# Hawk and RWKV layer on one core: normalized x of six sequences turned in squares of 32 on VectorE and spread by transfers inside SBUF

## The chip, the cores and the metric

The kernel runs on one core of a Trainium2 chip. The metric is the device time of one execution in microseconds (us). Three runs of the kernel before took 638.42, 637.23 and 638.24 us; their median is 638.24.

## The reference, cut to what matters

Everything is float32. The input x has 8 sequences of 1024 tokens with 256 features. It is normalized over the features, and two branches that both start from the normalized xn are added to x:

```python
xn = _layernorm(x, axis=-1)
x = x + hawk(xn, ...) + rwkv(xn, ...)

# hawk: 256 -> 384 features, and back
gate = xn @ Wg.T ;  u = xn @ Wi.T
y = causal_conv(u, 4 taps) + conv_b
ig = sigmoid(y @ lru_Wi.T + bi) ;  rg = sigmoid(y @ lru_Wg.T + bg)
alpha = exp(-8 * softplus(lam) * rg)
h[t] = alpha[t] * h[t-1] + sqrt(1 - alpha**2 + 1e-6) * ig * y      # along the tokens
hawk = (gelu(gate) * h) @ Wo.T

# rwkv: tokens mixed with the token before
xr = mu_r * xn + (1 - mu_r) * xn_prev ;  xk = mu_k * xn + (1 - mu_k) * xn_prev
rwkv = sigmoid(xr @ W_r.T) * (relu(xk @ W_k.T)**2 @ W_v.T)
```

## The kernel before

**Layout.** x arrives with tokens on the 128 partitions (`xt`, eight tiles of 128 tokens with 256 features). Statistics and normalization work on that layout, one token a partition. The products need the features on the partitions: `xnT` holds xn turned over, two chunks of 128 features with 1024 tokens each, behind one column of zeros, so that a view one column to the left is the token before. `mix_before` (ScalarE) and `mix` (VectorE) make the mixed inputs `xk` and `xr` from the two views.

**How xn is turned.** `transposes` (L681) lets TensorE turn four 128x128 blocks into one PSUM bank, and `put_transposed` copies the bank into `xnT` (ScalarE, L700; for one half of the first sequence's blocks VectorE). A sequence takes four banks, so 16 transposes and four copies. `tp` puts the four pairs into the order of the work.

**The products.** Each large product is done in 2x2 blocks with seven products in place of eight. For this GpSimd makes sums of token halves (`token_sum`, L712) and of weights, and five steps of a `Group` let TensorE, ScalarE (`seed`, `five`, evictions) and VectorE (`fork_c`, `fork_d`) take turns on the PSUM banks. Groups are u (gates and u, three of them), k, r, v (the rwkv branch), l (the gates of the recurrence, three) and o (the hawk output).

**The order.** There is one loop over the sequences, s = 0 to 7. A turn of the loop makes u, k, r, v and l of sequence s, finishes the recurrence and o of sequence s - 1, and prepares sequence s + 1. The order is written out by hand and by a planner: `pe(f, ...)` gives TensorE its next place on a counter (one place is the time of one float32 product with 512 columns, two matmul records in the trace), and `at(t, f, ...)` puts a step of another engine at a time in the same unit. Where the table `PLACES` has a name, its number replaces t. Its four parts are "first" (s = 0), "second" (s = 1), "middle" (s = 2 to 6) and "last" (s = 7). In the end all steps are sorted by that number and issued. The numbers are thus not times on the chip: they fix the order on each engine's queue, transfers included, and the hardware waits for data where a step comes early.

```python
def pe(f, *args, length=1):
    steps.append((clock[0], len(steps), f, args, ""))
    clock[0] += length
```

**Transfers.** SP issues the loads of x (`load`, L647), the early weights and the stores of the result (L638, L778). GpSimd issues `add_x` (L766), which adds x from HBM into the buffer `sides`. In a middle turn the kernel before has the load of sequence s + 2 directly behind the transposes of s + 1 (L681), since both use `xt`. The convolution steps on VectorE are L795, the forks L474 and L482, the normalization on ScalarE L676, `mix_before` L723 and `mix` L729.

Of the kernel before, what the change touches and what calls it, by code (L numbers as in the profile page):

```python
# [10 lines left out]
ALU = mybir.AluOpType  # L11

P = 128
NT = 512
K = 4
# [21 lines left out]
        "early mix_before k 0": 4.0, "early token_sum x 0": 4.88, "early token_sum x 2": 5.16,  # L37
        "early mix_before k 1": 5.2, "early mix k 0": 6.32, "u0_0 evict 0 1": 6.43,
        "early mix_before r 0": 7.11, "early token_sum x 1": 7.82, "u0_0 evict 1 1": 8.36,
        "early mix k 1": 8.98, "u1 seed": 9.36, "conv_first 1": 10.05, "early token_sum k 0": 10.48,  # L40
        "second stats 0 1": 10.52, "u2 seed": 11.39, "second stats 1 1": 11.39,
        "early token_sum x 3": 11.65, "u1 five": 12.07, "second stats 2 1": 12.26, "u2 five": 12.75,
        "early token_sum k 1": 12.81, "second stats 3 1": 13.13, "u1 evict A 0 0": 13.44,
        "early token_sum k 2": 13.97, "early mix_before r 1": 14.12, "u1 fork_c": 14.36,
        "early token_sum k 3": 15.13, "second stats 4 1": 15.17, "conv_first 0": 15.35,
        "early halve v": 16.29, "u2 fork_c": 16.36, "k seed": 17.36, "early mix r 0": 18.02,
        "u1 fork_d": 19.52, "u2 evict A 0 0": 19.54, "early token_sum r 0": 19.68,
        "second stats 5 1": 20.32, "u1 evict C 0 1": 20.36, "early weight_sums l": 20.85,
        "k five": 21.05, "u2 fork_d": 21.36, "conv_first 2": 21.73, "second stats 6 1": 22.17,
        "u2 evict C 0 1": 23.07, "k evict A 0 0": 23.75, "early constant 0": 24.44,  # L50
        "early mix r 1": 24.45, "u1 late": 24.7, "r seed": 25.37, "k fork_c": 25.93,
        "early constant 1": 26.05, "early token_sum r 1": 26.09, "r five": 26.36,
# [5 lines left out]
        "r fork_d": 34.36, "k evict C 0 1": 34.78, "conv_rest 0 2": 34.93, "normalize 0 1": 36.27,  # L58
        "conv_rest 1 1": 36.33, "conv_rest 0 3": 37.82, "r evict C 0 1": 38.46, "r evict A 0 0": 39.15,
        "conv_rest 2 1": 39.31, "r evict B 1 0": 39.82, "r late": 40.5, "token_sum y 0": 40.8,  # L60
# [3 lines left out]
        "normalize 7 1": 46.3, "value 0": 46.89, "token_sum y 1": 46.89, "value 4": 47.56,  # L64
        "token_sum y 2": 47.88, "l0 evict A 0 0": 48.22, "value 2": 48.3, "token_sum y 3": 49.02,
        "l0 fork_c": 49.36, "value 6": 50.17, "early constant 4": 50.97, "add_x": 51.13,
# [6 lines left out]
        "early constant 18": 55.58, "put_transposed 0 1": 56.15, "put_transposed 1 1": 56.83,  # L73
        "token_sum x 0": 57.0, "mix_before k 0": 57.52, "token_sum x 2": 58.16, "l0 evict B 1 0": 58.74,
        "mix k 0": 59.32, "mix_before k 1": 59.54, "l1 evict A 0 0": 60.77, "token_sum x 1": 60.82,
        "l1 fork_c": 61.36, "mix_before r 0": 61.57, "token_sum k 0": 61.98, "mix k 1": 63.14,
        "l2 seed": 63.36, "l2 five": 64.36, "token_sum x 3": 64.64, "l0 evict D 1 1": 65.05,
        "l1 fork_d": 65.36, "token_sum k 1": 65.81, "mix_before r 1": 65.84, "mix r 0": 66.97,
        "decay 0": 67.07, "l1 evict C 0 1": 68.41, "token_sum k 2": 68.47, "decay_square 0": 69.21,
        "token_sum k 3": 69.63, "l2 evict A 0 0": 70.32, "l2 fork_c": 70.36, "decay 1": 71.12,  # L80
        "mix r 1": 71.17, "l1 evict B 1 0": 72.47, "decay_rest 0": 72.66, "decay 2": 73.27,
        "stats 0 1": 73.47, "l2 fork_d": 74.36, "l1 evict D 1 1": 74.61, "stats 1 1": 75.17,
        "decay_square 1": 75.41, "l2 evict C 0 1": 76.52, "decay_square 2": 77.32, "stats 2 1": 77.42,
        "stats 3 1": 78.29, "stats 4 1": 79.16, "stats 5 1": 80.03, "decay_rest 1": 80.91,
        "decay_rest 2": 85.37, "stats 6 1": 97.23, "stats 7 1": 108.37
    },
    "second": {
        "token_sum r 0": -1.17, "gated_input 0": -0.0, "token_sum r 1": 1.42, "u0 seed": 2.43,
        "token_sum r 2": 2.58, "u0 five": 3.11, "token_sum r 3": 3.75, "beta 0": 5.29,
        "gated_input 1": 5.71, "u0 evict A 0 0": 6.52, "u0 fork_c": 7.14, "beta 1": 7.2,  # L90
        "scaled_input 0": 7.94, "l2 evict B 1 0": 9.93, "recur 0 L": 10.18, "l2 evict D 1 1": 10.73,
        "u1 seed": 11.53, "scaled_input 1": 11.63, "k seed": 12.21, "u1 five": 12.89,
        "u0 fork_d": 13.06, "u0 evict C 0 1": 13.58, "recur 0 R": 13.86, "k five": 14.26,
        "u1 evict A 0 0": 14.94, "gated_input 2": 15.32, "conv_first 0": 15.63, "u1 fork_c": 16.74,
        "k evict A 0 0": 16.97, "k fork_c": 17.55, "gated_state 0": 18.35, "beta 2": 19.15,
        "recur 1 L": 19.77, "u2 seed": 20.38, "u0 evict B 1 0": 21.06, "token_sum o 0": 21.23,
        "u2 five": 21.74, "u1 fork_d": 21.96, "u1 evict C 0 1": 22.43, "scaled_input 2": 22.76,
        "conv_first 1": 23.11, "k fork_d": 24.19, "conv_first 2": 24.45, "recur 2 L": 24.99,
        "k late": 25.8, "u2 fork_c": 26.45, "recur 1 R": 27.25, "u2 evict A 0 0": 27.98,
        "k evict C 0 1": 28.66, "recur 2 R": 28.71, "gated_state 1": 30.14, "r seed": 30.58,  # L100
        "r five": 31.26, "u2 fork_d": 31.57, "token_sum v 2": 31.57, "k evict B 1 0": 31.94,
        "token_sum o 1": 32.73, "u1 evict B 1 0": 33.73, "token_sum v 0": 33.89, "r fork_c": 34.27,
        "u2 evict C 0 1": 34.3, "token_sum o 2": 34.79, "r evict A 0 0": 34.82, "u2 evict B 1 0": 35.44,
        "gated_state 2": 35.88, "u1 late": 36.12, "u2 late": 36.8, "r fork_d": 37.29,
        "token_sum v 1": 37.29, "r evict C 0 1": 37.48, "v seed": 38.36, "conv_rest 0 1": 38.44,
        "r late": 39.04, "v five": 39.72, "token_sum v 3": 39.93, "r evict B 1 0": 40.4,
        "conv_rest 0 2": 41.08, "deviation": 42.56, "v fork_c": 42.57, "token_sum o 3": 42.57,
        "v evict A 0 0": 43.36, "o seed": 43.36, "conv_rest 0 3": 44.16, "o five": 44.36,
        "v fork_d": 45.65, "token_sum y 0": 45.81, "v evict C 0 1": 46.45, "conv_rest 1 1": 47.24,
        "inverse 0 8": 48.73, "normalize 0 1": 49.26, "o fork_c": 49.36, "normalize 1 1": 49.84,  # L110
        "conv_rest 2 1": 49.93, "normalize 2 1": 50.34, "normalize 3 1": 51.03, "conv_rest 1 2": 51.33,
        "normalize 4 1": 51.73, "normalize 5 1": 52.43, "o fork_d": 52.81, "normalize 6 1": 53.12,
        "conv_rest 2 2": 53.61, "normalize 7 1": 53.83, "l0 seed": 54.53, "conv_rest 1 3": 55.11,
        "l0 five": 55.36, "conv_rest 2 3": 56.6, "token_sum y 1": 57.87, "o evict B 1 0": 57.87,
        "token_sum y 2": 58.88, "o evict C 0 1": 59.3, "token_sum y 3": 60.02, "v evict B 1 0": 60.11,
        "l0 evict A 0 0": 60.72, "l0 fork_c": 60.91, "l1 seed": 62.36, "v late": 62.51, "add_x": 63.47,
        "put_transposed 0 0": 63.86, "put_transposed 1 0": 64.44, "l1 five": 65.01,
        "put_transposed 0 1": 65.69, "l0 fork_d": 66.36, "put_transposed 1 1": 66.38,
        "token_sum x 0": 66.54, "mix_before k 0": 67.06, "token_sum x 2": 67.7, "mix_before k 1": 68.29,
        "mix k 0": 68.87, "l0 evict C 0 1": 69.51, "mix_before r 0": 70.31, "token_sum x 1": 70.36,  # L120
        "mix k 1": 71.53, "l0 evict B 1 0": 71.54, "l1 evict A 0 0": 72.36, "token_sum k 0": 73.02,
        "mix_before r 1": 73.16, "l1 fork_c": 73.36, "mix r 0": 74.19, "l0 evict D 1 1": 74.39,
        "l2 seed": 75.36, "token_sum k 1": 75.68, "decay 0": 76.05, "mix r 1": 76.85, "l2 five": 77.39,
        "decay_square 0": 78.07, "token_sum x 3": 78.35, "l1 fork_d": 78.35, "decay 1": 79.18,
        "stats 0 1": 79.43, "token_sum k 2": 79.51, "stats 1 1": 80.3, "l1 evict C 0 1": 80.52,
        "token_sum k 3": 80.67, "stats 2 1": 81.17, "decay_square 1": 81.32, "l2 fork_c": 82.36,
# [1073 lines left out]
```

## Time and profile before

| | |
|---|---|
| median of 3 runs | 638.24 us |
| profiled execution | 638.32 us |
| its span, first to last instruction | 636.6 us |
| granted TensorE clock, mean | 0.999 |
| one turn of the loop (transposes at 137.05, 214.08, 291.11) | 77.03 us |
| HBM read, written | 19.94 MB, 8.39 MB |
| mean DMA rate over the span | 45 GB/s |

The profile shows one execution. Its times count from the first instruction. A group of instructions has the line, the engine, the operation, "out<-in", the count, busy time, the mean of one, and the idle time of the engine just before them with what ended it. In a timeline, "[1.13 <-PE bank L395]" means that the engine sat idle for 1.13 us until TensorE had written that bank. A "q" behind an engine's name is its queue of DMA issues. The chain follows the work that ended last back from the end, step by step, to what released it.

### The profile page before, as it was taken

The numbers are of one execution on the slowest core, as the hardware profiler recorded it, in microseconds if no ns is written. First come the engines' busy times: TensorE is split into PE (matmuls) and PEld (weight loads), VectorE is DVE, ScalarE is ACT, GpSimd is POOL, SyncE is SP. The second block draws the span as 40 slices with busy tenths as digits, with TensorE's granted clock in tenths as the row PEclk, the third lists the DMA queues.
The fourth block names the chain that finished last, engine by engine and source line by source line (L and its number), as shares of the span: only waits on it lengthen the run. The fifth ranks groups of instructions, "written<-read, shape, count | busy, mean of one in ns | idle before, by whom it ended". The sixth has DMA issues, their size and how long they took to land.

```text
span 636.6 us, 7412 instructions
## 1 busy us (share of the span) xinstructions
PE 628.3 (99%) x2632; PEld 379.3 (60%) x2632; DVE 510.1 (80%) x644; ACT 484.4 (76%) x693; POOL 328.0 (52%) x227
## 2 busy tenths in 40 slices
PE   9999999999999999999999999999999999999997
PEld 4466445964469544795447854487445974457466
DVE  4768697978889688886798867978789877689695
ACT  3995999669994699937999289981999739994870
POOL 5984833669044780547606475083831749617000
PEclk9999999999999999999999999999999999999999
DMA  7200500043000710008000070001700023000403
GB/s 265 67 1 9 124 0 1 1 103 97 0 1 1 154 45 2 0 1 199 0 1 2 30 169 0 0 2 42 158 0 1 1 75 58 0 2 1 66 28 106
DMA packets 27366, 28.80 MB, mean 45 GB/s; under 512 B 961, under 2 KB 26817, under 8 KB 27329
## 3 DMA queue, kind: packets, MB, share of 16 engines
q1 hardware_dynamic: 18592, 19.53, 9.6%
q0 software_dynamic: 8320, 8.39, 8.5%
q8 instruction: 21, 0.34, 0.2%
q10 hardware_dynamic: 416, 0.41, 0.2%
q14 instruction: 17, 0.13, 0.1%
HBM read 19.94 MB, written 8.39 MB: 44 GB/s over the span
## 4 chain that ended last, share of the span: by engine, by line
PE 95%; ACT 1%; DVE 0%; issue 0%; DVEq 0%; ACTq 0%
PE bank L389 65%; PE bank L395 24%; PE bank L739 4%; PE bank L681 2%; ACT g L555 0%; ACT L659 0%; ACT L555 0%; ACT L344 0%; DVE bank L474 0%; ACT bank L466 0%; ACT five L471 0%; DVE side L776 0%; DVEq L1195 0%; ACT std L659 0%; DVE std L666 0%
## 5 line engine op out<-in xcount | busy, mean ns | idle before, releaser
L389 PE MATMUL bank<-y,w_l 128*128 128x512 f32 x288 | 137.9, 593 | 0.0
L795 DVE SCALAR_TENSOR_TENSOR y<-u,par,y 128x1024 f32<-128x1024 f32 x72 | 105.4, 1490 | 0.2
L474 DVE TENSOR_TENSOR bank<-bank,five 128x512 f32<-128x512 f32 x76 | 52.9, 696 | 47.7 <-PE bank L389 28.5
L466 ACT COPY bank<-bank 128x512 f32<-128x512 f32 x76 | 44.1, 581 | 61.2 <-PE bank L389 57.0
L389 PEld LDWEIGHTS bank<-y,w_l 128*128 128x128 f32 x288 | 52.9, 190 | 58.7 <-issue 54.5
L389 PE MATMUL bank<-ysum,sum_l 128*128 128x512 f32 x144 | 72.0, 593 | 0.0
L389 PE MATMUL bank<-xsum,sum_u 128*128 128x512 f32 x138 | 69.3, 592 | 0.0
L712 POOL TENSOR_TENSOR tr<-g 128x512 f32<-128x512 f32 x12 | 17.0, 1418 | 85.7 <-DVE g L831 85.7
L712 POOL TENSOR_TENSOR ysum<-y,ysum 128x512 f32<-128x512 f32 x16 | 28.4, 1778 | 54.9 <-DVE y L795 54.9
L389 PE MATMUL bank<-xnT,w_u 128*128 128x512 f32 x108 | 54.1, 593 | 0.6 <-ACT xnT L700 0.6
L563 ACT ACTIVATE tr<-bank,half_b 128x512 f32<-128x512 f32 x48 | 33.2, 692 | 26.7 <-PE bank L389 26.7
L471 ACT COPY five<-bank 128x512 f32<-128x512 f32 x76 | 44.4, 586 | 5.0 <-PE bank L389 3.4
L389 PEld LDWEIGHTS bank<-ysum,sum_l 128*128 128x128 f32 x144 | 26.8, 190 | 31.5 <-issue 25.6
L712 POOL TENSOR_TENSOR tr<-g,tr 128x512 f32<-128x512 f32 x12 | 20.4, 1698 | 46.8 <-DVE g L831 46.8
L389 PEld LDWEIGHTS bank<-xsum,sum_u 128*128 128x128 f32 x138 | 25.6, 189 | 29.8 <-issue 28.1
L482 DVE TENSOR_TENSOR bank<-bank,five 128x512 f32<-128x512 f32 x30 | 20.7, 690 | 26.3 <-PE bank L389 26.3
L729 DVE SCALAR_TENSOR_TENSOR xk<-xnT,par,xk 128x1024 f32<-128x1024 f32 x16 | 33.7, 2142 | 7.9 <-ACT xk L723 7.9
L395 PE MATMUL bank<-w_o,g 128*128 128x128 f32 x288 | 37.0, 275 | 0.0
L395 PEld LDWEIGHTS bank<-w_o,g 128*128 128x128 f32 x288 | 35.0, 192 | 2.9 <-issue 2.9
L676 ACT ACTIVATE xt<-xt,mv,std 128x256 f32<-128x256 f32 x60 | 32.2, 593 | 5.0 <-DVE mv L667 4.5
L389 PEld LDWEIGHTS bank<-xnT,w_u 128*128 128x128 f32 x108 | 20.4, 190 | 25.9 <-issue 21.6
L822 DVE SCALAR_TENSOR_TENSOR ti<-ti,q 128x1024 f32<-128x1024 f32 (+1 forms) x25 | 33.1, 1329 | 2.8 <-ACT q L815 2.8
(165 smaller groups left out, 1507.9 us busy)
## 6 DMA issues: line engine op xcount, KB each, us to landing
side<-in_x_dram POOLq DMA_DIRECT2D x8, 1024.0 KB, 10.9
xt<-in_x_dram SPq DMA_DIRECT2D x7, 1024.0 KB, 9.7
out_dram<-side SPq DMA_DIRECT2D x12, 512.0 KB, 3.6
xt<-in_x_dram SPq DMA_DIRECT2D x4, 256.0 KB, 4.3
out_dram<-side SPq DMA_DIRECT2D x4, 256.0 KB, 2.1
out_dram<-side SPq DMA_DIRECT2D x8, 128.0 KB, 1.7
w_l<-in_lru_wg_dram SPq DMA_DIRECT2D x1, 576.0 KB, 5.9
w_l<-in_lru_wi_dram SPq DMA_DIRECT2D x1, 576.0 KB, 6.9
```

The costliest lines, as they stand in the source:

```text
L389: nc.tensor.matmul(banks[b], weight, tokens, start=start, stop=True, skip_group_check=True)
L395: nc.tensor.matmul(banks[b][:, p], tokens[:, p], weight, start=start and j == 0, stop=True, skip_group_check=True,)
L466: nc.scalar.copy(banks[bank["B"]], banks[bank["A"]])
L471: nc.scalar.copy(self.five, banks[bank["C"]])
L474: nc.vector.tensor_tensor(banks[bank["C"]], banks[bank["B"]], self.five, ALU.add)
L563: nc.scalar.activation(dst[:, m, HALVES[h]], src, AF.Tanh, bias=half_b[:, b + m : b + m + 1], scale=0.5)
L676: nc.scalar.activation(xa, xa, AF.Identity, bias=m, scale=r)
L712: nc.gpsimd.tensor_tensor(dst[o], a, b, ALU.subtract)
L729: nc.vector.scalar_tensor_tensor(dst, xnT[:, c, 1 : S + 1], column(MU[which] + c), dst, ALU.mult, ALU.add)
L739: nc.tensor.matmul(banks[b][:, j * D : (j + 1) * D], lhs[:, c, (t + j) * P : (t + j + 1) * P], families[w][:, c, :], start=(j == 0 and c = ...
L795: nc.vector.scalar_tensor_tensor(y[:, m, :], u[:, m, k : k + S], column(COL_CONV_W + k * HC + m), y[:, m, :], ALU.mult, ALU.add,)
L822: nc.vector.scalar_tensor_tensor(ti[:, m, p], ti[:, m, p], 0.5, q[:, m, p], ALU.mult, ALU.mult)
```

## The change

Sequences 0 and 1 are still turned by TensorE. For sequences 2 to 7 (`tp(s + 1)` in the turns s = 1 to 6) the following is put in its place:

- x is loaded by four transfers (`load_for_squares`), one for each 32 partitions, so that partition 32 i + c holds the tokens 256 i + 32 t + c, for t = 0 to 7. Statistics and normalization don't change.
- `squares` lets VectorE turn squares of 32x32 within each group of 32 partitions, four of the eight tiles at a time: two instructions over 128 x 1024 elements. They write into the buffer of `xk`, which is free then. Now partition 32 i + e holds feature e of each block of 32 features, for the tokens 256 i to 256 i + 255.
- `spread` moves this with sixteen transfers from SBUF to SBUF, one for each pair of a group i of source partitions and a group j of destination partitions. Each carries 32 partitions x 2 runs of 256 floats (64 KB), all issued by SP.
- `xnT` starts at column 32 instead of 1 (`X0`), and its columns before that are unused but for the zero at 31.

The PLACES of all turns are new, too. Normalization of the next sequence goes from places 35 to 43 to places 25 to 40, the squares stand at 33.12 and 43.16, the spreads from 44.74 to 51.02, the load behind them, the mixing from 56.29 (before: 67.06), and the statistics of the sequence after from 68.16 (before: 79.43). A turn counts 86 of TensorE's places instead of 88.

```diff
+BLOCK = 32
+X0 = BLOCK
...
-    xnT = fixed("xnT", [DC, S + 1])
+    xnT = fixed("xnT", [DC, X0 + S])
...
+    def load_for_squares(s):
+
+        n = P // BLOCK
+        for i in range(n):
+            rows = x[s, i * S // n : (i + 1) * S // n, :].rearrange("(t c) d -> c t d", c=BLOCK)
+            nc.sync.dma_start(xt[i * BLOCK : (i + 1) * BLOCK], rows)
...
+    def squares(s, t):
+
+        src = xt[:, t : t + 4, :].rearrange("p t (k e) -> p t k e", e=BLOCK)
+        dst = turned_home()[:, :, t : t + 4, :].rearrange("p k t e -> p t k e")
+        nc.vector.transpose(dst, src)
+
+    def turned_home():
+
+        flat = mixes["k"].rearrange("p a b -> p (a b)")
+        return flat.rearrange("p (k t e) -> p k t e", t=TT, e=BLOCK)
+
+    def spread(s, i, j):
+
+        n = P // BLOCK
+        src = turned_home()[i * BLOCK : (i + 1) * BLOCK].rearrange("c (k j) t e -> c k j (t e)", k=DC)[:, :, j]
+        dst = xnT[j * BLOCK : (j + 1) * BLOCK, :, X0 + i * S // n : X0 + (i + 1) * S // n]
+        nc.sync.dma_start(dst, src)
...
+    def turned(t, s):
+        for n in range(2):
+            at(t + 2 * n, squares, s, 4 * n)
+        for i in range(P // BLOCK):
+            for j in range(P // BLOCK):
+                at(t + 4 + i / 10 + j / 100, spread, s, i, j)
+        if s + 1 < B:
+            load_next(t + 5, s + 1)
+
+    def load_next(t, s):
+        at(t, load_for_squares, s)
+        for a in range(TT):
+            at(t + 12 + a, stats, s, a, 1)
...
             if not last:
                 for t in range(TT):
-                    at(b + (36 if first else 41) + t, normalize, s + 1, t, 1)
+                    at(b + (36 if first else 20) + t, normalize, s + 1, t, 1)
+                if not first:
+                    turned(b + 28, s + 1)
...
             if not last:
                 if first:
                     ls[0].step(3)
-                tp(s + 1)
-                if s + 2 < B:
-                    at(now() + 1, load, s + 2, 0, TT)
-                    for t in range(TT):
-                        at(now() + 11.3 + t, stats, s + 2, t, 1)
-                token_sums(now() + 1.5, s + 1, "x")
-                mixing(now() + 2, now() + 5, "k")
-                token_sums(now() + 8.2, s + 1, "k")
-                mixing(now() + 4.6, now() + 8.2, "r")
+                    tp(1)
+                    load_next(now() + 1, 2)
+                late = 1.5
+                token_sums(now() + late, s + 1, "x")
+                mixing(now() + late + 0.5, now() + late + 3.5, "k")
+                token_sums(now() + late + 6.7, s + 1, "k")
+                mixing(now() + late + 3.1, now() + late + 6.7, "r")
```

In the places of a middle turn, VectorE's order between 31 and 60 (c for a convolution step):

```diff
-u2 fork_d, inverse, r fork_c, c, r fork_d, c, c, v fork_c, v evict A, c, v fork_d, v evict C, c, o fork_c, c, c, o fork_d, c, c, o evict A
+u2 fork_d, squares 0, r fork_c, c, r fork_d, c, c, v fork_c, squares 4, c, v fork_d, c, v evict A, o fork_c, c, v evict C, o fork_d, c, c, c, o evict A
```

## The prediction

> **What bounds the kernel now.** I read the page first, for the busy shares and the chain that ended last.
>
> ```profile
> PE 628.3 (99%) x2632; PEld 379.3 (60%) x2632; DVE 510.1 (80%) x644; ACT 484.4 (76%) x693; POOL 328.0 (52%) x227
> PEclk9999999999999999999999999999999999999999
> PE 95%; ACT 1%; DVE 0%; issue 0%; DVEq 0%; ACTq 0%
> PE bank L389 65%; PE bank L395 24%; PE bank L739 4%; PE bank L681 2%; ACT g L555 0%; ACT L659 0%; ACT L555 0%; ACT L344 0%; DVE bank L474 0%; ACT bank L466 0%; ACT five L471 0%; DVE side L776 0%; DVEq L1195 0%; ACT std L659 0%; DVE std L666 0%
> ```
>
> TensorE is busy 99% of the span at a full granted clock, and 95% of the chain is its products, one behind the other. The transposes that the change takes away (L681) are 2% of the chain themselves. Whatever leaves TensorE's queue therefore shortens the run, as long as no other engine becomes late in its place. Next I read the chain in order of time in one middle turn of the loop.
>
> ```profile
> 264.91 0.86 PE bank L389 x2
> 265.77 0.09 issue
> 265.87 16.55 PE bank L395 x144
> ...
> 291.11 1.77 PE bank L681 x16
> ```
>
> Sixteen transposes of one sequence hold TensorE for 1.77 us, with work directly before and behind them; the only gap in the turn is 0.09 us. The same piece comes at 214.08 and 137.05, so a turn lasts 77.03 us. This turn's first product starts at 235.43; I count its time from there ("turn time"), and 88 places of TensorE fill it, 86 after the change.
>
> **What is removed.** Six turns (the second to the seventh) lose 16 transposes: 6 x 1.77 = 10.62 us of the chain. ScalarE loses four evictions of about 0.60 us a turn, 2.4 us, which were off the chain. The profiled execution took 638.32 us (span 636.60 and 1.72 around it): 638.32 - 10.62 = 627.70. The median of the runs shown, 638.24, is 0.08 lower, so it goes to 627.6 if everything added is covered.
>
> **The two squares on VectorE.** No transpose on VectorE is in this trace. These rows (by form: busy, mean ns) bound one over 128x1024 f32.
>
> ```profile
> L812 DVE TENSOR_SCALAR q<-q 128x1024 f32<-128x1024 f32 x24 | 19.3, 808 | 4.3 <-ACT q L809 4.3
> L831 DVE TENSOR_TENSOR g<-g,q 128x1024 f32<-128x1024 f32 x21 | 25.3, 1229 | 0.0
> L729 DVE SCALAR_TENSOR_TENSOR xk<-xnT,par,xk 128x1024 f32<-128x1024 f32 x16 | 33.7, 2142 | 7.9 <-ACT xk L723 7.9
> ```
>
> The ends are 0.68 us (the quickest L812) and 2.41 (the slowest L729, beside GpSimd). I take 1.21: the row that moves one element after another and is undisturbed is the nearest to an instruction that must pass each element through. Next is where they lie, read from VectorE's timeline.
>
> ```profile
> 262.31 0.69 DVE L482 TENSOR_TENSOR g<-bank,five 128x512 f32<-128x512 f32 x1 [0.16 <-PE bank L389]
> ...
> 265.02 0.70 DVE L474 TENSOR_TENSOR bank<-bank,five 128x512 f32<-128x512 f32 x1 [1.71 <-ACT side L615]
> ...
> 272.46 0.70 DVE L474 TENSOR_TENSOR bank<-bank,five 128x512 f32<-128x512 f32 x1 [1.13 <-PE bank L395]
> ...
> 282.31 2.47 DVE L795 SCALAR_TENSOR_TENSOR y<-u,par,y 128x1024 f32<-128x1024 f32 x2
> ```
>
> Square 0 is put between the fork at 262.31 and r's fork at 265.02. The first is done at 262.92; the reciprocal that stood there moves forward, so 2.10 us are free. TensorE reads r's fork at once (its next product is the one at 265.87), so each us beyond 2.10 is a us of the run. The square also needs four normalizations from ScalarE: they are brought to places 25 to 32, and ScalarE ran half a place ahead of its written places here (r's eviction, written 34.27, came at place 33.6), so I expect the fourth at about 263.4 and the square done at 264.6.
>
> Square 4 goes behind the fork at 272.46, in front of the last six convolution steps. Those ended at 284.78. Who waits for them is read from GpSimd and TensorE:
>
> ```profile
> 283.76 2.16 POOL L712 TENSOR_TENSOR ysum<-y,ysum 128x512 f32<-128x512 f32 x1 [8.82 <-DVE y L795]
> ```
>
> ```profile
> 285.75 1.88 PE L389 MATMUL bank<-y,w_l 128*128 128x512 f32 x4
> 287.47 1.02 PE L389 MATMUL bank<-ysum,sum_l 128*128 128x512 f32 x2
> ```
>
> The third chunk of y is used at 286.6, 1.8 us after it was ready; the token sum that ends at 285.92 is used at 287.47, 1.55 later. With 0.31 us of idleness inside the stretch, 1.86 us can be added before TensorE feels it. At a cost C a square the stall is max(0, C - 2.10) + max(0, C - 1.86) a turn: nothing at 1.21, 0.31 + 0.55 = 0.86 at 2.41, and all of the 1.77 is eaten only at C = 2.87. The Trainium skill speaks against the move: "VectorE: DVE Perf Modes", section "The three transpose paths", gives VectorE 311 ns for a 128x128 block in bf16, in blocks of 32 only, and advises TensorE for whole 128x128 ones. By that figure a square of eight such blocks would be an estimated 2.49 us, the stall 1.02 a turn, and the run 627.6 + 6.1 = 633.7. The trace has 1.77/16 = 0.11 us for a block on TensorE, but that engine is the bound and VectorE has 20% free.
>
> **The sixteen transfers and the load.** All are issued by SP, which here issues nothing between 215.92 and 286.71. Issue and landing are read from SP's timeline and the page's DMA issues:
>
> ```profile
> 0.73 1.98 SPq L647 DMA_DIRECT2D xt<-in_x_dram  x4
> ```
>
> ```profile
> xt<-in_x_dram SPq DMA_DIRECT2D x4, 256.0 KB, 4.3
> out_dram<-side SPq DMA_DIRECT2D x8, 128.0 KB, 1.7
> ```
>
> A chain of issues costs 0.50 us apiece (1.98/4), or 0.69 by the weight loads at 2.75 and 3.44; a 64 KB transfer lands 1.7 us behind (nearest row 128 KB), 4.3 at most. The transfers also read and write SBUF on both sides, which no row shows. Square 4 ends at 273.07 + 1.21 = 274.28, turn time 38.85. Sixteen issues of 0.50 and 1.7: the last lands at 48.6; with 0.69 and 4.3 at 54.2. Its first reader is `mix_before` on ScalarE, at place 56.29, turn time 49.7. ScalarE's timeline says what a wait costs there:
>
> ```profile
> 275.19 0.62 ACT L555 ACTIVATE g<-g 128x512 f32<-128x512 f32 x1
> 283.31 0.57 ACT L466 COPY bank<-bank 128x512 f32<-128x512 f32 x1 [7.50 <-PE bank L389]
> ...
> 293.97 2.23 ACT L723 ACTIVATE xk<-xnT,mu_rest 128x1024 f32<-128x1024 f32 x2
> ```
>
> Before, the mixing began at turn time 58.5 and ScalarE had 7.5 us of nothing at 40 to 48. Behind the first `mix_before` after the change stand two more, one eviction, the last `mix_before` and l1's seed: 1.18 + 1.18 + 1.16 + 0.69 + 1.16 + 0.58 = 5.95 us. TensorE needs that seed at place 70, 61.5. So the transfers may land until 55.5 at no cost; the cover holds at both ends. Once it is gone, each us is a us.
>
> The load for the sequence after becomes four issues behind the spreads: 38.85 + 20 x 0.50 + 9.7 (a 1024 KB load's landing) = 58.6, or 62.4 by the dear issues. The first statistics stand at 59.9. At the dear end VectorE waits 2.5 us, with three more statistics and l1's fork behind it; TensorE needs that fork at 64.9 and gets it at 65.2, 0.3 a turn or 1.9 in all. The two stores of `out` come behind these issues instead of before the load and may go out a little over 1 us late; nothing waits for them until their buffer is written a turn later. "DMA: Bandwidth & Descriptors", section "Bandwidth", calls transfers under 64 KB bound by descriptors and advises 1 MiB; these are 64 KB. Its 0.95 us for such a one on the engines would put sixteen, strictly one after another, at an estimated 38.85 + 15.2 = 54.1, still before 55.5.
>
> The new buffers' owners are out of the way: `xk`, which holds the squares, is last read by TensorE at place 28, and `xnT` at place 32. `add_x` moves four places back on GpSimd's queue; its transfer (10.9 us) ends near turn time 69, and its buffer is needed in the next turn.
>
> The shift of `xnT` to column 32 I price at nothing: products from `xnT` and from `y` both take 593 ns. The new written order puts the other steps of ScalarE, VectorE and GpSimd within a few us of where they were; adding 2.4 us of VectorE to a turn of 75.26 keeps it at about 85% by the page's 80%.
>
> **The rivals.**
> - Dear squares: 2.0 to 2.6 us each. For it: L729 and L795 reach 2.41 and 2.35 beside GpSimd. Against it: a square reads one input, and one-input rows (L812) go down to 0.68. Stall 0.1 to 1.2 a turn: 628.5 to 635; at 2.41, 632.8. Still faster.
> - Late transfers (slower): SP needs more than 1.05 us for each, because an issue waits for an earlier landing. From (57.3 - 38.85 - 1.7)/16 = 1.05 on, ScalarE's stalled evictions cost TensorE over 1.77 a turn. At 1.2 us the last lands at 59.8: 4.3 lost, 1.77 gained, 6 x 2.5 = 15 longer: 653. For it: one early load of weights sat 0.6 us behind another load's landing, and such a wait could chain. Against it: stretches of issues here go at 0.5 to 0.69.
> - The square isn't one instruction but one for each 32 columns: 32 x 0.16 (L351, VectorE's smallest row) = 5.1 us, stall 3.0 + 3.2, less 1.77, six times: 665. The diff shows one call on a whole view, which speaks against it.
>
> **How the numbers follow.** Covered: 0.62. Dear squares: 0.12, faster too. Stalls that happen to eat the gain to within 0.2% (1.3 us, about what a measurement can tell): 0.04. Late transfers: 0.17. Split squares: 0.05. So faster 0.74, same 0.04, slower 0.22. The forecast is 627.6; its own range is 626 (the 0.09 us gaps gone, and 1 us below the median as the quickest run before) to 630 (the load's 1.9). For 8 in 10 I add the dear squares, the unchanged case and the first of the late transfers: 626 to 641.
>
> **What would show it.** Right: no L681 piece in the turns from the second on, a turn of 75.3 us, squares near 1.2 us, the last spread landed near turn time 49, at most 2 us of ScalarE waiting before `mix_before`. Wrong: idle TensorE before r's products (square 0 or its normalizations late), before `ysum` products (square 4), or before l1's second step (transfers); statistics waiting long for the load.

## The result

The changed kernel takes 628.21 us (median of four runs, 627.36 to 629.47) beside 638.00 us for the kernel before (four runs, 637.23 to 638.42): a ratio of 0.985, 95% interval 0.9827 to 0.9872. The forecast was 627.6. The profiled execution of the changed kernel took 629.47 us, the longest of the four; its span is 627.7, with 1.77 around it.

The busy shares, the granted clock and the chain of the page after:

```profile
PE 618.2 (98%) x2536; PEld 368.8 (59%) x2536; DVE 525.1 (84%) x656; ACT 471.4 (75%) x667; POOL 321.7 (51%) x227
PEclk9999999999999999999999999999999999999999
PE 89%; DVE 3%; SPq 2%; ACT 1%; DMA 1%; issue 1%; POOL 0%; DVEq 0%; POOLq 0%; ACTq 0%
```

TensorE has 96 matmul records less (2632 to 2536) and 10.1 us less of work. It still leads, but 3% of the chain is now VectorE's and 2% SP's issues. Before, those were 0. To see where, I split the span at the same piece of each turn (columns: stretch and its length, busy time of each engine, granted clock, DMA share, GB/s):

```profile
111.61:189.21 77.60, 75.69 (x322) 45.34 (x323) 67.67 (x81) 59.56 (x87) 39.95 (x28) 1.00 0.25 55
189.21:264.53 75.32, 75.23 (x323) 45.43 (x323) 66.00 (x80) 58.30 (x84) 39.00 (x26) 1.00 0.25 57
264.53:339.85 75.32, 75.24 (x323) 45.42 (x323) 65.99 (x80) 58.36 (x84) 38.99 (x26) 1.00 0.25 56
```

The next three turns are 75.30, 75.31 and 75.32. Before, each of the six was 77.02 to 77.04. Five turns thus save 1.71 or 1.72 us each, 8.57 in all. The second turn lasts 0.56 longer than before, 2.28 longer than its neighbours. The first turn's end comes 0.19 sooner, and the last stretch is 0.70 shorter, of which 0.59 is the final store's landing. That makes 8.57 - 0.56 + 0.19 + 0.70 = 8.90, and the spans are 636.60 and 627.7.

In a middle turn, the two squares on VectorE's timeline, then SP's spreads and load, then the first reader of the spread data on ScalarE:

```profile
262.17 1.25 DVE L722 STREAM_TRANSPOSE xk<-xt 128x1024 f32<-128x1024 f32 x1 [0.44 <-ACT xt L691]
263.68 0.70 DVE L482 TENSOR_TENSOR bank<-bank,five 128x512 f32<-128x512 f32 x1 [0.27 <-PE bank L403]
271.73 1.23 DVE L722 STREAM_TRANSPOSE xk<-xt 128x1024 f32<-128x1024 f32 x1
```

```profile
273.11 10.47 SPq L734 DMA_DIRECT2D xnT<-xk  x16
283.67 2.04 SPq L665 DMA_DIRECT2D xt<-in_x_dram  x4
```

```profile
285.30 2.19 ACT L756 ACTIVATE xk<-xnT,mu_rest 128x1024 f32<-128x1024 f32 x2 [1.82 <-DMA xnT<-xk]
```

A square takes 1.24 us, and r's fork behind the first one still waits 0.27 us for TensorE, not TensorE for it. Sixteen spreads are issued in 10.47 us (0.65 apiece); over the six turns it is 10.28 to 11.64 (0.64 to 0.73). ScalarE waits 1.82 us for the last landing, 1.42 to 2.81 over the six turns, and no product of this turn waits. The turn's first product starts at 234.16, so the mixing begins at turn time 51.1.

### The profile page after: what moved, and what is told of

Same layout as the page of the kernel before. It is cut to its first block, busy times and chain, and to the rows that moved or that the text cites. A ratio compares the mean times of both kernels' runs of the same rounds, so it can differ in the third digit from the quotient of the medians.

```text
span 627.7 us, 7452 instructions
## 1 busy us (share of the span) xinstructions
PE 618.2 (98%) x2536; PEld 368.8 (59%) x2536; DVE 525.1 (84%) x656; ACT 471.4 (75%) x667; POOL 321.7 (51%) x227
## 4 chain that ended last, share of the span: by engine, by line
PE 89%; DVE 3%; SPq 2%; ACT 1%; DMA 1%; issue 1%; POOL 0%; DVEq 0%; POOLq 0%; ACTq 0%
PE bank L397 62%; PE bank L403 22%; PE bank L772 4%; SPq L734 1%; DMA out_dram<-side 1%; DVE xk L762 1%; DVE q L845 1%; DVE bank L482 0%; DVE st L669 0%; SPq L665 0%; PE bank L696 0%; ACT g L563 0%; DVE xr L762 0%; POOL ysum L745 0%; ACT L674 0%
## 5 line engine op out<-in xcount | busy, mean ns | idle before, releaser
L828 DVE SCALAR_TENSOR_TENSOR y<-u,par,y 128x1024 f32<-128x1024 f32 x72 | 103.0, 1456 | 0.2
L482 DVE TENSOR_TENSOR bank<-bank,five 128x512 f32<-128x512 f32 x76 | 52.7, 694 | 36.1 <-PE bank L397 25.6
L745 POOL TENSOR_TENSOR tr<-g 128x512 f32<-128x512 f32 x12 | 21.1, 1755 | 84.1 <-ACT u L559 71.9
L745 POOL TENSOR_TENSOR xsum<-ysum 128x512 f32<-128x512 f32 x12 | 16.0, 1354 | 66.3 <-PE bank L403 58.3
L571 ACT ACTIVATE ti<-bank,half_b 128x512 f32<-128x512 f32 x48 | 31.5, 683 | 7.4 <-PE bank L397 7.2
L691 ACT ACTIVATE xt<-xt,mv,std 128x256 f32<-128x256 f32 x60 | 33.6, 596 | 1.0 <-DMA w_o<-in_w_o_dram 0.6
L852 DVE SCALAR_TENSOR_TENSOR ti<-ti,y 128x1024 f32<-128x1024 f32 (+1 forms) x25 | 30.5, 1239 | 4.3 <-ACT ti L571 4.3
L845 DVE TENSOR_SCALAR q<-q 128x1024 f32<-128x1024 f32 x24 | 32.9, 1390 | 1.3 <-ACT q L842 1.2
```

The costliest lines, as they stand in the source:

```text
L482: nc.vector.tensor_tensor(banks[bank["C"]], banks[bank["B"]], self.five, ALU.add)
L571: nc.scalar.activation(dst[:, m, HALVES[h]], src, AF.Tanh, bias=half_b[:, b + m : b + m + 1], scale=0.5)
L691: nc.scalar.activation(xa, xa, AF.Identity, bias=m, scale=r)
L745: nc.gpsimd.tensor_tensor(dst[o], a, b, ALU.subtract)
L828: nc.vector.scalar_tensor_tensor(y[:, m, :], u[:, m, k : k + S], column(COL_CONV_W + k * HC + m), y[:, m, :], ALU.mult, ALU.add,)
L845: nc.vector.tensor_scalar(q[:, m, :], q[:, m, :], -1.0, 1.0, ALU.mult, ALU.add)
```

## The experiments

**Is TensorE's removed time the whole gain?** Sixteen transposes of a block of `w_v` go back into TensorE's queue in each of the six turns; their output is read by nobody.

```diff
+    def idle_transposes():
+        for n in range(4):
+            for t in range(4):
+                nc.tensor.matmul(banks[free[0]][:, t * P : (t + 1) * P], families["v"][:, 0, 0:P], ident, is_transpose=True, ...)
...
+                if not first:
+                    pe(idle_transposes, length=0)
```

> The changed kernel with sixteen transposes of a weight block put back on TensorE in the six turns, at the old place; nobody reads their results and every other queue keeps its order. Theory (the gain is TensorE's removed time and nothing else): 6 x 1.77 = 10.6 us longer than the changed kernel, about 638.8, no other wait. Rival (the new written order of the other engines gave the gain, TensorE had room): at most 630.

Measured: 638.09 us (637.70 to 638.46, ten runs), ratio to before 1.0005 [0.9996, 1.0014]. All of the gain is gone. With TensorE's time restored, the squares, the spreads and the freed copies of ScalarE leave nothing measurable in total. Single turns still differ: in the profile the second turn is 0.57 us longer than in the kernel before and the sixth 0.36, while the last stretch is 0.73 shorter. The second turn lasts 77.61 us here and 77.60 in the first profile of the changed kernel: there TensorE waited, and the removed transposes gained nothing.

**How much room have the squares?** Each is done twice.

```diff
         nc.vector.transpose(dst, src)
+        nc.vector.transpose(dst, src)
```

> Each square is done twice, the second time over the first: a square costs 2 x 1.24 = 2.48 us of VectorE. Theory (VectorE has room of about 2.1 us at square 0 and 1.9 at square 4): a stall of 0.38 + 0.62 = 1.0 us a turn at TensorE, ahead of r's products and of the token sums of y; about 634. Rival (VectorE is already at its limit, every us added is a us lost): 12 x 1.24 = 14.9 longer, 643. Second rival (plenty of room): 628.

Measured: 635.43 us (635.04 to 637.58), ratio 0.9966 [0.9957, 0.9976]. That is 7.2 us over the changed kernel, 1.20 a turn for 2 x 1.24 us more of VectorE. The list of waits has the place, TensorE's r and o products behind the forks that follow the squares (columns: total us, times, longest):

```profile
PE bank L403 <- DVE bank L482: 9.5, 12, 1.4
```

The two rooms together are 4 x 1.24 - 1.20 = 3.76 us, where the prediction had 2.10 + 1.86 = 3.96. One by one they fit less well. The waits in one middle turn:

```profile
266.48 2.02 PE L403 MATMUL bank<-sum_r,xr 128*128 128x128 f32 x16 [0.93 <-DVE bank L482]
280.51 1.13 PE L403 MATMUL bank<-sum_o,tr 128*128 128x128 f32 x8 [0.40 <-DVE bank L482]
```

The expectation had 0.38 us ahead of r's products and 0.62 ahead of the token sums of y. By these waits the first room is about 1.6 us (2.48 less 0.93), the second about 2.1, and behind square 4 the first reader that is late is o's fork, not the token sums.

**How much cover have the spreads?** Eight or sixteen more 64 KB transfers, from `xk` to a buffer that nobody reads, are issued ahead of the sixteen.

```diff
+    spare = fixed("spare", [DC, S // 4])
+    def spread_spare(s, i, j):
+        src = ...                       # as in spread
+        nc.sync.dma_start(spare[j * BLOCK : (j + 1) * BLOCK], src)
...
+        for m in range(8):              # 16 in the second kernel
+            at(t + 4, spread_spare, s, m // 4, m % 4)
```

> Eight more transfers of 64 KB into a spare buffer ahead of the sixteen: at 0.64 us an issue the last spread lands and the load goes out 5.1 us later. Theory (cover until turn time 55.5, the last landed near 50.5 now): the first mix_before starts at about 56, TensorE hardly waits for l1's seed; the late load makes VectorE wait some us ahead of the statistics and costs TensorE 0.5 to 1.5 us a turn: 631 to 637. Rival (transfers are at no path at all): 628. Rival (no cover, each us counts): 628 + 6 x 5.1 = 659.

> Sixteen more transfers of 64 KB ahead of the sixteen: spreads and load 10.3 us later. Theory: the cover of some 5 us is used up, l1's seed on ScalarE comes about 5 us late and l1's fork on VectorE, behind the statistics, about 6: 5.5 to 6.5 us a turn, 661 to 667. Rival (no path): 628. Rival (no cover): 628 + 6 x 10.3 = 690.

Measured: 653.94 us (648.39 to 655.14) with eight, ratio 1.0237 [1.0193, 1.0281]; 689.42 (687.33 to 690.34) with sixteen, 1.0806 [1.0784, 1.0827]. The cover was far smaller than predicted. The waits of the kernel with eight:

```profile
DVE bank L490 <- ACT tr L571: 26.3, 6, 4.7
PE bank L397 <- DVE bank L490: 17.2, 6, 3.2
```

The late reader isn't l1's seed, which the prediction took, but l0's `fork_d` on VectorE. It writes a PSUM bank that l0's first eviction on ScalarE has to give back, and that eviction stands behind three `mix_before` in ScalarE's queue. In one turn `mix_before` began 5.07 us later than in the changed kernel (both counted from the first of that turn's transfers on SP) and TensorE waited 2.53: the cover is 2.5 us. In the same turn of the kernel with sixteen, TensorE waited 7.63, again 2.5 less than twice 5.07. The profiled run with eight was 648.4 us; what the longer runs of it add, up to 6.8 us, was not profiled. Their mean granted clock is 0.987 to 0.992, beside 0.997 in the profiled run. Lost clock is thus a likely part of it (an estimate: 0.010 of 648 us is 6.5 us); the last section shows where clock is lost.

**Is that bank the only path?** The same kernel with eight more transfers, and l0's first eviction moved ahead of the mixing.

```diff
-"mix_before k 0": 56.29, "mix_before k 1": 57.51, "mix_before r 0": 58.74, "l0 evict A 0 0": 59.96
+"l0 evict A 0 0": 59.36, "mix_before k 0": 59.37, "mix_before k 1": 59.38, "mix_before r 0": 59.39
```

> The kernel with eight more transfers (653.9 us), with l0's first eviction put ahead of the three mixing steps on ScalarE in the six turns. Theory (the 4.3 us a turn came from l0's second fork, which waits for the PSUM bank that this eviction gives back, and the eviction sat behind the mixing): the wait ahead of that fork goes, and what is left is l1's seed and the statistics, at most 1.5 us a turn: 629 to 637. Rival (late data themselves, through xnT and the load, hold up TensorE): still about 650.

Measured: 656.39 us (653.62 to 656.55), ratio 1.0278 [1.0256, 1.03]. `fork_d` no longer waits for the eviction, but TensorE waits at the next readers, l1's seed on ScalarE and the forks behind VectorE's mixing, 22.5 us in all beside 17.2 at the fork before:

```profile
PE bank L397 <- DVE bank L482: 12.7, 7, 2.4
PE bank L397 <- ACT bank L474: 9.8, 6, 2.0
```

So the bank is the first reader of late data, not the only one. The order of ScalarE's queue moves the wait and doesn't remove it.

**What costs the second turn its 2.3 us?** TensorE waits there twice, and VectorE's first mixing step of k (L762) takes 3.79 us; undisturbed ones take 1.25.

```profile
146.75 1.12 PE L397 MATMUL bank<-ysum,sum_l 128*128 128x512 f32 x2 [0.47 <-DVE bank L482]
156.17 1.12 PE L397 MATMUL bank<-ysum,sum_l 128*128 128x512 f32 x2 [1.42 <-DVE bank L482]
```

In the second turn statistics stand between the mixing steps; in the middle turns they stand behind. First I moved the two steps ahead of them.

```diff
-"mix k 0": 65.89, ... "mix k 1": 69.86      # places of the second turn
+"mix k 0": 65.05, ... "mix k 1": 65.1
```

> In the second turn alone both mixes of xk stand ahead of the first statistics on VectorE, as in the middle turns. Theory (that turn loses 2.3 us in the profiled execution because VectorE takes the mix late, beside GpSimd's add_x, and everything behind it comes late): the turn goes from 77.6 to 75.3 us, the runs lie at 626 to 627.5 and no longer up to 629.5. Rival (that turn is slow because its spreads are issued late): 627.4 to 629.5 as before.

Measured: 628.45 us (627.80 to 628.83), ratio 0.9852 [0.9839, 0.9866]: no effect that can be told from the changed kernel. The two steps together took 6.12 us, and the turn 76.49. Next to them GpSimd issues the transfer that adds x (`add_x`, L799), so the next theory was that issue. Three kernels ran on one chip: the changed kernel again, one with `add_x` behind the last token sum of x, and one with both moves.

```diff
-"add_x": 65.47
+"add_x": 67.4
```

> The changed kernel once more, on the chip of the next run: 627.4 to 629.5 us, with the second turn at 77.6 us and its first mixing step of k on VectorE at about 3.8 us.

> Only the place of one GpSimd instruction changes: in the second turn the transfer that adds x to the output rows is issued after the last token sum of x instead of ahead of it. Theory (the second turn's 2.3 us over the middle turns come from VectorE's first mixing step of k, 3.79 us instead of 1.3 to 2.7, beside this issue): the step takes 1.3 to 2.2 us, TensorE's two waits of 0.47 and 1.42 us on VectorE's copies go, the turn takes 75.3 to 76.0 us and the kernel 626.0 to 626.8. Rival (the late spreads and the late load set the turn, the issue is only beside it): step or not, the turn stays within 0.3 of 77.6 us and the kernel at 627.4 to 629.5.

> The later issue of the adding transfer, and with it the first two mixing steps of k ahead of the statistics on VectorE in the second turn. Theory (the issue): as with the later issue alone or up to 0.5 us better, 625.6 to 626.8 us, since the step then also starts some 0.6 us sooner. Rival (late spreads): 627.4 to 629.5.

Measured: 627.61 us (627.32 to 628.91) for the changed kernel again, ratio 0.9844 [0.9831, 0.9858]; 628.67 (628.28 to 629.33) with the later issue, 0.9858 [0.9845, 0.9872]; 627.49 (627.12 to 628.00) with both moves, 0.984 [0.9826, 0.9853]. The changed kernel didn't repeat its second turn: 76.06 us instead of 77.60, with a first step of 1.46. The theory falls, too: with the issue moved away the first step took 1.45 us, but the second took 3.51. Timelines of the second turn from three profiles show what blocks it. The changed kernel, first profile:

```profile
140.32 1.90 POOL L745 TENSOR_TENSOR xsum<-xnT,xsum 128x512 f32<-128x512 f32 x1
139.53 3.79 DVE L762 SCALAR_TENSOR_TENSOR xk<-xnT,par,xk 128x1024 f32<-128x1024 f32 x1
```

The changed kernel, second profile:

```profile
138.97 1.46 DVE L762 SCALAR_TENSOR_TENSOR xk<-xnT,par,xk 128x1024 f32<-128x1024 f32 x1
141.53 1.85 POOL L745 TENSOR_TENSOR side<-xk 128x512 f32<-128x512 f32 x1
141.96 2.52 DVE L762 SCALAR_TENSOR_TENSOR xk<-xnT,par,xk 128x1024 f32<-128x1024 f32 x1
```

With the later issue:

```profile
142.64 1.91 POOL L745 TENSOR_TENSOR side<-xk 128x512 f32<-128x512 f32 x1
142.13 3.51 DVE L762 SCALAR_TENSOR_TENSOR xk<-xnT,par,xk 128x1024 f32<-128x1024 f32 x1
```

The long step ends 1.10 us after GpSimd's token sum (143.32 and 142.22; 144.48 and 143.38) and 1.09 in the last one (145.64 and 144.55). It is 1.10 too in the kernel with mixing first (144.77 and 143.67) and in the one with `xnT` at column 1, further down (143.33 and 142.23). A step alone takes 1.25. The reading that fits all five is that the step is held until GpSimd's instruction has ended and then does nearly all of its own work. In the second profile the issue of `add_x` (139.30 to 140.86) was over before the long step began, so a token sum alone can hold it. In the middle turns it goes the other way: GpSimd's first sum of k takes 2.23 us there, and the steps 1.50 and 1.27.

With the order of the changed kernel, the end of the second step then sets the turn. The time from it to the next turn's start is 43.12, 43.11, 43.13 and 43.13 us (the changed kernel twice, later issue, and column 1 below), while the turns themselves last 77.60, 76.06, 77.06 and 75.70 us. In the kernels with the mixing first it is 43.56 and, with both moves, 44.78, so there something else decides. The two profiles of the changed kernel differ by 1.7 us of span, and 1.54 of it is this turn; that its runs scatter between 627.3 and 629.5 for the same reason is likely, but only two of them were profiled. Of the 1.54, the first step's later start makes 0.48. In the first profile the statistics ahead of that step waited 0.37 us for the load of x, and the chain that ended last runs through SP's spreads and load there. Late transfers, the rival, thus have a part in that profile, and no run separates it. With both moves the turn is 75.91. That kernel's runs overlap with those of the changed kernel, so it isn't shown to be better.

Last, `add_x` was put ahead of the token sums of x.

```diff
-"add_x": 65.47
+"add_x": 61.1
```

> One place changes: in the second turn GpSimd issues the transfer that adds x ahead of the four token sums of x, some 4 us before VectorE's mixing steps of k, instead of between the last two sums. Theory (the second turn lasts 43.1 us past the end of the second mixing step of k, which was so in four profiles to 0.02 us, and the steps are long only near this issue): the two steps take 2.6 to 3.4 us together instead of 5.0 or 4.0, the second ends 31.6 to 32.4 us after the turn's start, the turn takes 75.3 to 75.6 us and the kernel 626.9 to 627.5 us. Rival (the steps are long because the token sums of x run beside them, not the issue): the sums now end 1 us later, the steps still take 4 to 5 us, the turn 76.1 to 77.6 us, the kernel 627.4 to 629.5 us.

Measured: 637.69 us (636.87 to 639.15), ratio 1.0001 [0.9992, 1.0011]. The place was badly chosen. `add_x` adds into the buffer that the v products are multiplied into, and there it stands ahead of the last of them: x is multiplied in as well, and that quarter of the sequence's output comes out wrong. VectorE's product waits for the whole transfer:

```profile
146.46 0.69 DVE L634 SCALAR_TENSOR_TENSOR side<-side,five 128x512 f32<-128x512 f32 x1 [10.84 <-DMA side<-in_x_dram]
```

It doesn't decide between issue and sums, since by then both were over. The two steps, with GpSimd idle, took 1.28 and 1.25 us.

**Does the shift to column 32 cost anything?** `xnT` begins at column 1 again.

```diff
-X0 = BLOCK
+X0 = 1
```

> xnT starts at column 1 again instead of 32; all else as changed. Theory (column priced at nothing, TensorE is the bound): within 1 us of 628. Rival (the spreads, and VectorE's and GpSimd's reads of xnT, need the aligned column: mixes back from 1.4 to 2.1 us, spreads slower): the mixing comes late enough for TensorE to wait, 632 or more.

Measured: 628.60 us (626.60 to 629.42), ratio 0.9851 [0.9834, 0.9868]: nothing that can be told from the changed kernel. Products from `xnT` take 592 ns, and an issue of a spread has a median of 595 ns.

**Would the seventh turn of TensorE's transposes pay too?** Sequence 1 goes by squares and spreads as well, in the first turn, with that turn's places shifted by hand and the mixing first in the second turn.

```diff
-                if not first:
-                    turned(b + 28, s + 1)
+                turned(b + 28, s + 1)
...
-                    tp(1)
-                    load_next(now() + 1, 2)
+                    clock[0] += 2
```

> e4_mix_first, and sequence 1 is turned by squares and spreads too, its squares behind the convolution of the first turn, its mixing some ten places later. Theory (TensorE's removed time is the gain wherever the other engines have room): another 1.8 us less than e4_mix_first, 624 to 626. Rival (the late mixing pushes ScalarE and VectorE into the dense second turn): 626 to 632.

Measured: 638.70 us (637.64 to 639.62), ratio 1.0015 [1.0006, 1.0024]. The spreads were issued from 60.31 to 74.76 us and the mixing fell to 76 to 87 us, without slack in the queues behind; between 62 and 109 us TensorE is busy for 41.04 us and the granted clock is 0.93, beside 47.00 and 1.00 in the changed kernel. The second turn lasts 76.50 us, as with the mixing first alone (76.49), so the loss lies ahead of it. The forecast and its rival both missed. It fits that the gain needs a stretch where SP and ScalarE have time; whether a better order would win here stays open.

## Why the prediction was right, and where its steps were off

The total was right to 0.6 us, by its main step: TensorE is the bound, and what leaves its queue shortens the run as long as the rest is hidden. Putting the transposes back shows that, in total, nothing else moved the time. The parts, in the order of the prediction:

- **Removed work.** 1.77 us a turn predicted, 1.71 measured in five turns.
- **The second turn.** Not foreseen. The prediction costed one middle turn and multiplied by six, though the second turn has a table of places of its own. It gained -0.56 in one profile and 0.98 in the other. That the total fits nevertheless is partly compensation: the start and the last stretch gave 0.89 and 1.03 us in the two profiles, which were not in the sum.
- **Squares.** 1.21 predicted, 1.24 measured (1.233 to 1.246); the room of 3.96 us is 3.76. Its split was off: about 1.6 and 2.1 us, predicted 2.10 and 1.86, and the reader named for the second, the token sums of y, isn't the one that becomes late. That the sum fits is partly luck. The estimate of 2.49 us from the bf16 figure in the Trainium skill's "VectorE: DVE Perf Modes", section "The three transpose paths", was twice the measured time of this float32 instruction, and the measurement decides. Doubled squares took the run to 635.43; the prediction's 633.7 for a square of 2.49 us is near it.
- **Spreads.** 0.50 us an issue was too cheap; it is 0.64 to 0.73, about the dear end of 0.69. They land 2.0 us behind, predicted 1.7. So the mixing began at turn time 51.1, predicted 49.7 (dear end 54.2). ScalarE waits 1.8 us for it in that turn, but more than the "at most 2" in four of the six.
- **Cover of the spreads.** This step failed, though without effect on the time. The prediction followed ScalarE's queue only to l1's seed and gave the transfers until 55.5. The first reader of the delay is l0's `fork_d`, through a PSUM bank that an eviction behind the mixing gives back; the limit is 51.1 + 2.5 = 53.6. "The cover holds at both ends" was thus wrong: the dear end, 54.2, lies behind it. The rival of late transfers begins at (53.6 - 38.9 - 2.0)/16 = 0.79 us a transfer and eats the gain at 0.90, not at 1.05. At 0.64 to 0.73 the kernel is nearer to it than the prediction said.
- **Load and statistics.** The first statistics of a middle turn start at 294.02, turn time 59.86 (predicted 59.9), with no wait.
- **VectorE's share.** About 85% predicted, 84% measured over the span. A middle turn, for which the 85% was worked out, has 88% (66.0 of 75.32 us).

## What to carry to other kernels

When the bound engine has no gaps, work that leaves its queue is worth its full time, and the question is only whether the substitute keeps inside the rooms of the other queues: read those from the timeline, reader by reader, and follow each delayed queue through the buffers that it gives back, not only through the data that it makes. Cost each kind of turn that has an order of its own, the first ones above all. When an instruction takes much longer than its kind, compare its end with the ends of the instructions on the other engines before blaming what stands beside its start.

## What the hardware showed

VectorE's step with two inputs in SBUF and GpSimd's token sum don't run side by side: one waits for the whole of the other, and VectorE's ended 1.09 to 1.10 us behind GpSimd's in five profiles. The Trainium skill's "SBUF — State Buffer", section "Who interferes with whom", says this: a VectorE instruction with two SBUF inputs and a GpSimd instruction that reads SBUF contend for a port that only one of them can hold, and the order of issue decides which one blocks. What decides here who goes first stays open. Steps that began 0.07 and 0.16 us after the start of the `add_x` issue took 1.28 and 3.79 us, both ahead of the recorded start of the next sum.

A long idle time of TensorE costs more than itself. In the kernel with sixteen more transfers, after the wait of 7.63 us:

```profile
319.39 2.04 PE L397 MATMUL bank<-ysum,w_l 128*128 128x512 f32 x2 [7.63 <-DVE bank L490]
321.23 4.46 PE L397 MATMUL bank<-y,w_l 128*128 128x512 f32 x6
```

Eight records took 6.14 us up to the next at 325.53, with a granted clock of 0.50 between 320 and 324 us; in the changed kernel the same eight took 3.43 (292.24 to 295.67). After the wait of 2.53 us they took 3.51, at a clock of 1.00. The Trainium skill's "TensorE: Matmul & The Clock Gate", section "What's actually happening", has half the clock after an idle window of about 3.4 us, which these two waits agree with. Shorter waits in other runs don't. In the kernel with the eviction first:

```profile
318.59 1.49 PE L397 MATMUL bank<-ysum,sum_l 128*128 128x512 f32 x2 [2.40 <-DVE bank L482]
319.88 1.91 PE L397 MATMUL bank<-y,sum_l 128*128 128x512 f32 x2
```

The clock was 0.50 between 320 and 322 us, and the six records up to the next at 322.97 took 4.38 us; in the changed kernel the same six took 2.65 (306.83 to 309.48). Another wait of 2.40 us in that kernel was followed by slow products too, and so was one of 3.17 in the second turn with eight more transfers; waits of 2.41 and 3.20 us in the same two kernels were not. So a wait of 2.4 us can already cost half the clock for some microseconds. What decides it between 2.4 and 3.2 us isn't shown.
